# From attention to gating in a four-layer image kernel: `w1` and image 0's first norm moved ahead of a branch, cross terms in one instruction, three more places for image loads

## The chip, the cores and the metric

The kernel runs on one core of one Trainium2 chip. The core has a matrix engine (TensorE, PE in the profile), a vector engine (VectorE, DVE), a scalar engine (ScalarE, ACT), GpSimd (POOL) and a sync engine (SyncE, SP) that issues most of the transfers between device memory (HBM) and the core's own memories: SBUF for operands, and PSUM, into which PE writes its products. Each engine runs its own list of instructions in order, and waits on semaphores for the others. The metric is the device time of one execution in microseconds (us). All tensors are f32.

## The reference, cut to what matters

The input `x` is 8 images of 384 channels of 32x32 points. Four layers follow each other, and each adds its result to its input; a group norm `_gn` (32 groups of 12 channels, per image) stands ahead of each layer.

```python
x = x + _L0(_gn(x))     # attention; ends with a batch norm over all 8 images
x = x + _L1(_gn(x))     # gated layer: 4 experts
x = x + _L2(_gn(x))     # depthwise and pointwise convolution with ternary weights
x = x + _L3(_gn(x))     # deformable attention

# layer 0, the end
out = einsum('bhnm,bhcm->bhcn', attn, v)
out = einsum('oc,bchw->bohw', w_out, out)
return (out - m) * rsqrt(v + EPS) * g + b      # m, v: of each channel, over all images

# layer 1
scores = softmax(x_flat @ gate_w + gate_b, -1)       # 4 experts for every point
top_v, top_i = top_k(scores, 2)
top_w = softmax(top_v, -1)
wmap = top_w.T.reshape(2, b, h, w)
present = (top_i[:, :, None] == arange(4)[None, None, :]).any(0)
coef = einsum('ke,kbhw->ebhw', present, wmap)
hdn = relu(einsum('bchw,edc->ebdhw', x, w1) + b1)
y = einsum('ebdhw,eod->ebohw', hdn, w2) + b2
out = einsum('ebohw,ebhw->bohw', y, coef)
```

Two things follow from this. The batch norm of layer 0 needs the projected output of all eight images, so the group norm of layer 1 can't be had for any image before the last attention product is done. And `present` is taken over all points of all images: the gates of all images must be known before any expert's coefficient is.

## The kernel before

**Tiles.** The 384 channels are 3 chunks of 128 partitions, the 1024 points are a row, taken in two halves of 512 (`HALF`). [...]`x` and the attention's projected output `o` lie in HBM; an image's `x` or `o` in SBUF takes 1.57 MB, and five such places exist (pool `im`, L209).

**The attention stage** (L672 to L951) goes through the images, head pairs and halves. For each image, `out_project` (L746) multiplies by `w_out` (tile `wo0`), copies the product `po` to `ot`, takes its statistics (`bn_stats` into `ost`) and stores it to `o`; it also loads `xh`, the same half chunk of `x`. `cross` (L665) then takes the sum over points of (x - mean of x) times o: a multiply of two tensors on DVE, and a sum over its result (L668); for the second half, `moments` puts the statistics together. From mean and variance of x (`xmv`), of o (`omv`) and the cross term (`xo`), the group statistics of x + batch norm(o) can be worked out without another pass over the data. The last image's second half is projected at the end of the stage (tiles `pos`), its crosses come last (`ends`). During the last image, five image tiles are loaded ahead (`fetch`, L723): x and o of images 0 and 1, and x of image 2.

**The range test** (L942 to L951). `rec` holds the 1024 columns of reciprocals of the softmax sums. One test of all of them against two bounds gives a flag, `bad`; a product with ones (`pok`) adds it up over partitions.

**The norms** (`norms`, L966 to L1002). In order on DVE, with POOL and PE in between: the batch norm's scale and shift (`bn_params`, L159; the reciprocal root is one POOL instruction, `rsqrt`, L98), the channel means summed, a product that spreads them over each group (`gmean`, L976), the channel variances summed, a second such product (`gvar`, L993), POOL's reciprocal root for all eight images, and `rs1`, `sf1`, `sb1`, scale and shift of the norm for each image and channel.

**The branch** (L1007). Every engine loads the flag `bad` and branches: where the range test failed, everything in the If (L1008 to L1140) computes the attention again in an exact manner. With this input the If is skipped. PSUM is handed from the attention's pools to the gated layer's behind it.

**The gated layer's first part.** Behind the branch come `w1` (2.36 MB) and `b1` (L1180, by `load_w`, issued at L1150), the join of image 0 (`join`, `attended`, L1223: x + o times scale, three DVE instructions of 128x1024), and image 0's hidden products. `layer1` (L1417) makes the work for one image as a list of `units`: `enter` (L1431) applies the norm to one half (ScalarE; tile `h1`, shown as `h`), `hidden` (L1495) makes three products `ph` (L1499) for each of 12 k and relu (L1509). The list is interleaved with the loads and joins of the other seven images and with `logits` (L1234), which multiplies each pair of images by the gate (`plog`, L1239). The gate weights themselves, scaled by each image's norm, are built by `gating` (L1203).

**What sets the order.** A scheduler orders each engine's instructions by priorities that follow the order of the program text, unless `issue_after` holds an instruction behind another. SP has one in-order list: a transfer whose place is not free holds up all that are issued behind it. The image loads are issued by `fetch_next` (L1250) from a list, one or two at a time, into whichever of the five places comes free; `w2`, `b2` and the weights of layer 3 (`wq3`, `wk3`, `wv3` and smaller ones) are issued behind the last image load.

**The second part.** With all logits, `route` (L1255) makes the two softmaxes and `present` on DVE, the weights go through HBM (`w0d` out, `w0s` back as a row over all partitions, in `spread`, L1450), `coefficients` and `weight` (L1477) make the coefficient tile `cb` on ScalarE and multiply the hidden tiles by it on DVE (L1485), and `result` (L1514) makes the products `y` (L1520) and adds them to x. Two of the three chunks of the second half's normed input (`h1` in `enter`) lie in the two places of `cb`, so a coefficient tile can only be written when the hidden products no longer read them.

Then the images' layers 1 to 3 follow, in which PE is busy throughout.

Of the kernel before, what the change touches and what calls it, by code (L numbers as in the profile page):

```python
# [13 lines left out]
N = H * W  # L14
# [41 lines left out]
def tile_kernel(ctx: ExitStack, tc: tile.TileContext, i: dict, out: bass.AP):  # L56
# [102 lines left out]
    def bn_params(g, b, tiles):  # L159

        mv, sc, sh = tiles
        n = mv.shape[1]
        nc.vector.tensor_scalar(sh, mv[:, :, 1], 1e-5, None, ALU.add)
        rsqrt(sc, sh, n)
        nc.vector.tensor_tensor(sc, sc, g, ALU.mult)
        nc.vector.tensor_tensor(sh, mv[:, :, 0], sc, ALU.mult)
        nc.vector.tensor_tensor(sh, b, sh, ALU.subtract)
        return sc, sh
# [496 lines left out]
    def cross(b, m, h, xh, ot):  # L665

        nc.vector.scalar_tensor_tensor(xh, xh, xmv[:, b, m, 0:1], ot, ALU.subtract, ALU.mult)
        nc.vector.reduce_sum(xo[:, b, m, h : h + 1], xh, AX.X)  # L668
        if h == 1:
            moments(omv[:, b, m, :], ost[:, m, 2 * b : 2 * b + 2, :])  # L670

    with ExitStack() as pb:  # L672
# [73 lines left out]
        def out_project(b, m, h, po=None):  # L746
            hs = slice(h * HALF, (h + 1) * HALF)
            xh = op.tile([P, HALF], F32, tag="xh", name=f"xh{b}_{m}_{h}")
# [13 lines left out]
            ot = op.tile([P, HALF], F32, tag="ot", name=f"ot{b}_{m}_{h}")  # L762
# [8 lines left out]
            cross(b, m, h, xh, ot)  # L771

        def spare(k, h):


            vf = vts[B % 2].rearrange("p t h d -> p (t h d)")
# [91 lines left out]
        for n, (b, pr, h, kc) in enumerate(steps):  # L868
            if kc == 0:
# [9 lines left out]
                if b + 1 == B and pr == 3 and h == 0:  # L879
                    for k in range(3, 5):  # L880
                        fetch(k)
                if b + 1 == B and pr == 2 and h == 1:
# [42 lines left out]
        for k in range(2):  # L925
            qs = slice(k * HALF // 2, (k + 1) * HALF // 2)
            for m in range(KC):
                for c in range(KC):
# [3 lines left out]
                    )  # L932
        ends = [out_project(B - 1, m, 1, pos[m]) for m in range(KC)]
        for m in range(KC):
            first = bn_moments(ost, m, sc_o)
        ends[0]()

        with tc.issue_after(first.ins):
            for end in ends[1:]:
                end()  # L940

        okt = pp.tile([P, B * NU * 16], F32, tag="p", name="okt")  # L942
        recf = rec.rearrange("p u q -> p (u q)")
        with tc.issue_after(turned.ins):
            nc.vector.tensor_scalar(okt, recf, R_LO, None, ALU.is_ge)
        nc.vector.scalar_tensor_tensor(okt, recf, R_HI, okt, ALU.is_le, ALU.mult)
        okm = np_.tile([P, 1], F32, tag="okm", name="okm", bufs=1)
        nc.vector.tensor_reduce(okm, okt, AX.X, ALU.min)
        pok = bank("pok")
        nc.tensor.matmul(pok[:, 0:1], lhsT=ones, rhs=okm, start=True, stop=True)  # L950
        nc.vector.tensor_scalar(bad, pok[:, 0:1], P - 0.5, None, ALU.is_lt)  # L951
# [3 lines left out]
    w0_ctx.close()  # L955
    _, sco, sho = sc_o
    rs1 = const.tile([P, B], F32, name="rs1")
    sf1 = const.tile([P, B], F32, name="sf1")
    sb1 = const.tile([P, B, KC], F32, name="sb1")
    mean_c = const.tile([P, B, KC], F32, name="mean_c")  # L960
    var_c = const.tile([P, B, KC], F32, name="var_c")
    xs_c = const.tile([P, B, KC], F32, name="xs_c")
    sum_g = const.tile([P, B], F32, name="sum_g")
    mean_g = const.tile([P, B], F32, name="mean_g")

    def norms(moments):  # L966
        for c in range(KC if moments else 0):
            bn_moments(ost, c, sc_o)
        bn_params(gbo[:, 0, :], gbo[:, 1, :], sc_o)
        sc, sh = (t.unsqueeze(1).to_broadcast([P, B, KC]) for t in (sco, sho))  # L970
        nc.vector.tensor_tensor(mean_c, omv[:, :, :, 0], sc, ALU.mult)
        nc.vector.tensor_tensor(mean_c, mean_c, xmv[:, :, :, 0], ALU.add)
        nc.vector.tensor_tensor(mean_c, mean_c, sh, ALU.add)
        nc.vector.reduce_sum(sum_g, mean_c, AX.X)
        pg = bank("gmean")
# [1426 lines left out]
```

## Time and profile before

| | us |
|---|---|
| runs (three) | 3414.34, 3416.99, 3419.63; median 3416.99 |
| profiled execution | 3421.18, its span 3419.1 |
| PE busy | 3321.6 (97%) |
| DVE busy | 1776.3 (52%) |
| ACT busy | 1299.8 (38%) |
| POOL busy | 204.1 (6%) |

HBM is read for 146.33 MB and written for 75.59 MB. The mean granted clock of PE is 0.991 of full speed.

Times below are us from the start of the span. In the list of groups, a row names the line, the engine, the operation, what it writes and reads, the shape, and how many; then the busy time, the mean of one in ns, and, behind the second bar, the idle time of the engine just before these instructions with what ended most of it. In the list of waits, a row says which group of instructions waited for which, and then the sum of the waits in us, their number, and the longest. "SPq" or "DVEq" is the sequencer of an engine, "issue" a time in which an engine waited for nothing that the profile shows. Records of a branch carry the line of the If (L1008).

### The profile page before, as it was taken

To read this page: it belongs to the slowest core of one execution; us is meant where nothing else is said; L and a number is where in the kernel's file an instruction comes from. 1 tells how busy PE (TensorE), PEld (TensorE's weight loads), DVE (VectorE), ACT (ScalarE), POOL (GpSimd) and SP (SyncE) were. 2 spreads that over 40 slices of the span, in tenths; PEclk is the share of its full clock that TensorE was granted. 3 is DMA by queue.
4 is the path that set the end of the run, shared out by engine and by line. 5 is a ranking of instruction groups with operands and counts; after the bars stand their busy time and mean duration, and the time that the engine had idled before them with its cause. 6 is when DMAs were issued, how large, how long until landed. Compare 5 with 4: busy or idle time off the path is not lost.

```text
span 3419.1 us, 44835 instructions
## 1 busy us (share of the span) xinstructions
PE 3321.6 (97%) x18479; PEld 1440.5 (42%) x18479; DVE 1776.3 (52%) x2982; ACT 1299.8 (38%) x1519; POOL 204.1 (6%) x237
## 2 busy tenths in 40 slices
PE   6989999999999999999799999999999999999989
PEld 2433434343434343434344444444444444444444
DVE  8852232323232323234466585565855658658765
ACT  4655444444444444434112332223322232222341
POOL 2110000000000000000000110201102011020121
PEclk9999999999999999999899999999999999999999
DMA  9983121212121111112710010101101011010000
GB/s 355 292 230 81 26 81 26 73 34 66 41 58 49 54 52 50 57 46 74 291 58 22 36 40 27 58 28 36 40 29 57 28 36 40 33 53 27 0 19 38
DMA packets 86979, 234.56 MB, mean 69 GB/s; under 512 B 21880, under 2 KB 22104, under 8 KB 79850
## 3 DMA queue, kind: packets, MB, share of 16 engines
q1 hardware_dynamic: 84602, 223.30, 20.4%
q10 hardware_dynamic: 1248, 4.72, 0.4%
q8 instruction: 149, 2.44, 0.3%
q0 software_dynamic: 912, 3.53, 0.3%
q14 instruction: 68, 0.56, 0.0%
HBM read 146.33 MB, written 75.59 MB: 65 GB/s over the span
## 4 chain that ended last, share of the span: by engine, by line
PE 49%; DVE 2%; ACT 0%; DMA 0%; POOL 0%; issue 0%; DVEq 0%; SPq 0%; POOLq 0%; ACTq 0%
PE y L1520 14%; PE ph L1499 14%; PE pf L2030 4%; PE pq L1682 3%; PE pw L1653 3%; PE pav L1902 3%; PE s L1876 2%; PE pk L1847 1%; DVE off L1778 1%; PE pv L1858 1%; PE xsb L1828 1%; PE pw_last L2091 1%; PE xs L1828 0%; PE px L1742 0%; PE plog L1239 0%; PE pom L1709 0%
## 5 line engine op out<-in xcount | busy, mean ns | idle before, releaser
L827 ACT ACTIVATE p<-s 128x1024 f32<-128x1024 f32 x512 | 496.3, 1021 | 365.7 <-PE s L820 365.5
L1499 PE MATMUL ph<-h,w_sb 128*128 128x512 f32 x1104 | 490.0, 599 | 15.5 <-DMA b_sb<-in_b_dram 14.9
L835 PE MATMUL pav<-p,vt 64*64 64x512 f32 x4096 | 494.9, 588 | 0.0
L1520 PE MATMUL y<-hd,w_sb 128*128 128x512 f32 x1080 | 485.4, 597 | 2.2 <-DVE hd L1485 2.2
L820 PE MATMUL s<-qk,qk 48*64 48x512 f32 x2944 | 355.3, 592 | 0.0
L1499 PEld LDWEIGHTS ph<-h,w_sb 128*128 128x128 f32 x1104 | 208.9, 191 | 273.6 <-issue 270.1
L1520 PEld LDWEIGHTS y<-hd,w_sb 128*128 128x128 f32 x1080 | 199.2, 190 | 233.2 <-issue 221.2
L796 DVE COPY ta<-pav 128x512 f32<-128x512 f32 (+1 forms) x65 | 44.3, 682 | 475.0 <-PE pav L835 475.0
L835 PEld LDWEIGHTS pav<-p,vt 64*64 64x64 f32 x4096 | 168.9, 133 | 272.8 <-issue 272.8
L1509 ACT ACTIVATE hd<-ph,b_sb 128x512 f32<-128x512 f32 x180 | 122.6, 681 | 267.1 <-PE ph L1499 267.1
L574 PE MATMUL pk<-xs,cws_sb 32*32 32x496 f32 (+3 forms) x3840 | 179.6, 604 | 41.0 <-DMA xs<-in_xs_dram 24.7
L1778 DVE SCALAR_TENSOR_TENSOR off<-q,dw_sb,off 128x225 f32<-128x225 f32 (+4 forms) x441 | 215.5, 543 | 2.6
L1641 DVE SCALAR_TENSOR_TENSOR y<-h,tap,y 128x961 f32<-128x961 f32 (+1 forms) x168 | 203.2, 1230 | 0.5
L820 PEld LDWEIGHTS s<-qk,qk 48*64 48x64 f32 x2944 | 109.6, 133 | 210.9 <-issue 190.0
L81 DVE COPY qk<-pq 128x512 f32<-128x512 f32 x46 | 31.8, 692 | 251.9 <-PE pq L258 251.9
L1893 ACT ACTIVATE p<-s 128x1024 f32<-128x1024 f32 x96 | 93.4, 1021 | 161.8 <-PE s L1876 152.6
L1485 DVE TENSOR_TENSOR hd<-hd,cb 128x512 f32<-128x512 f32 x180 | 122.6, 686 | 46.4 <-ACT hd L1509 37.9
L574 PEld LDWEIGHTS pk<-xs,cws_sb 32*32 32x32 f32 (+1 forms) x3840 | 78.4, 111 | 140.6 <-issue 54.6
L1962 POOL TENSOR_TENSOR p<-p,p 128x1024 f32<-128x1024 f32 x48 | 113.7, 2368 | 325.2 <-ACT p L1893 266.8
L2030 PE MATMUL pf<-att,wp_sb 128*128 128x512 f32 x288 | 131.3, 601 | 0.0
L820 PE MATMUL s<-ql,ql 48*64 48x512 f32 x1024 | 128.4, 592 | 0.2 <-ACT p L827 0.2
L711 PE MATMUL pv<-wv_sb,g 128*128 128x384 f32 x384 | 127.1, 489 | 0.0
(369 smaller groups left out, 3744.6 us busy)
## 6 DMA issues: line engine op xcount, KB each, us to landing
rqk<-y SPq DMA_DIRECT2D x96, 256.0 KB
g<-rqk SPq DMA_DIRECT2D x96, 256.0 KB
xs<-in_xs_dram SPq DMA_DIRECT2D x56, 384.0 KB
g<-rv SPq DMA_DIRECT2D x48, 256.0 KB
xh<-in_x_dram SPq DMA_DIRECT2D x48, 256.0 KB
f<-in_x_dram SPq DMA_DIRECT2D x24, 512.0 KB
f<-o SPq DMA_DIRECT2D x24, 512.0 KB
o<-ot SPq DMA_DIRECT2D x42, 256.0 KB
```

The costliest lines, as they stand in the source:

```text
L574: nc.tensor.matmul(banks[r][cols[q]].rearrange("p (h w) -> p h w", w=W)[:, :, c0:c1], lhsT=cws[rs, c, 2 * h + g, x, w], rhs=src[rs, :, c0 ...
L711: nc.tensor.matmul(pv[:, :C], lhsT=acts[b][2][:, c, t * P : (t + 1) * P], rhs=w_in[2][:, c, :], start=(c == 0), stop=(c == KC - 1),)
L820: nc.tensor.matmul(s[64 * k : 64 * k + 64, j * HALF : (j + 1) * HALF], lhsT=kt[r, k0 : k0 + 64], rhs=qt[r, h * HALF : (h + 1) * HALF], sta ...
L827: nc.scalar.activation(p, s, AF.Exp, scale=scale)
L835: nc.tensor.matmul(pav[k][64 * j : 64 * j + 64, :], lhsT=vts[b % 2][r, kc, 2 * hd : 2 * hd + 2, :].rearrange("p a b -> p (a b)"), rhs=p[r, ...
L1485: ahead["hd"] = nc.vector.tensor_tensor(hd, hd, state["cb"], ALU.mult)
L1499: ahead["ph"] = nc.tensor.matmul(ph, lhsT=w1[:, e, c, dc * P : (dc + 1) * P], rhs=state["h1"][c], start=(c == 0), stop=(c == KC - 1),)
L1509: nc.scalar.activation(hd, ph, AF.Relu, bias=b1[:, k : k + 1])
L1520: nc.tensor.matmul(y, lhsT=w2[:, e, dc, m * P : (m + 1) * P], rhs=state[h, k], start=(k == 0), stop=(k == NE * KC - 1),)
L1641: nc.vector.scalar_tensor_tensor(d, f, tap2[:, c, t : t + 1], d, ALU.mult, ALU.add)
L1778: nc.vector.scalar_tensor_tensor(d, f, dw3[:, t : t + 1], d, ALU.mult, ALU.add)
L2030: nc.tensor.matmul(pf, lhsT=wp3[:, pr, m * P : (m + 1) * P], rhs=att[:, pr, hs], start=(pr == 0), stop=(pr == NPAIR3 - 1),)
```

## The change

The edits, in the order of the diff:

- `bn_params` returns its first instruction, so that others can be placed behind it. `cross` becomes one instruction with a second output, the sum over its columns (`accum_out`); `cross_end` adds the `moments`.
- `norms` becomes a generator that stops at points where other work can be placed. It computes all eight images up to the group variance, and then only image 0's `rs1`, `sf1`, `sb1`; `norms_left` does the other seven, behind the branch. The tiles move up to the constants.
- In the last half's projection, the third chunk's `xh` and `ot` lie in memory that is free by then (the attention output of image 6, and a `p` tile). `spare`, another user of free memory, also moves there from a value tile.
- The range test is cut in two: `in_bounds(0)` takes the 896 columns of images 0 to 6, at the second head pair of image 7; `in_bounds(1)` takes the last 128 columns. `pok` adds both.
- The last crosses are placed: cross 0 behind the first instruction of `bn_params`, crosses 1 and 2 behind the sum of means.
- Ahead of the branch: a new pool `h` with `w1` (four transfers), `b1` and the first half's normed image 0 (`h_first`); the first half of image 0's join, one chunk behind each of the variance's sum, the addition of epsilon, and the last instruction of the norm; and the norm itself (`enter_first`). If the If is entered, it does these again. The gated layer's PSUM pools are opened ahead of the branch too, and the If uses them.
- Behind the branch: `join` of image 0 takes the second half only; image loads get named places, the five `im` tiles and three more: `w2`'s memory, the memory of `wq3`, `wk3`, `wv3`, and the three `flat` tiles. Two tables (`NEXT`, `BEHIND`) say which load is issued where. `w2` is loaded behind the last image load as before; `wq3`, `wk3` and `wv3` are loaded behind `w0s`, in the second part.

```diff
@@ bn_params
-        nc.vector.tensor_scalar(sh, mv[:, :, 1], 1e-5, None, ALU.add)
+        begun = nc.vector.tensor_scalar(sh, mv[:, :, 1], 1e-5, None, ALU.add)
...
-        return sc, sh
+        return begun
@@ cross
-        nc.vector.scalar_tensor_tensor(xh, xh, xmv[:, b, m, 0:1], ot, ALU.subtract, ALU.mult)
-        nc.vector.reduce_sum(xo[:, b, m, h : h + 1], xh, AX.X)
+        nc.vector.scalar_tensor_tensor(
+            xh, xh, xmv[:, b, m, 0:1], ot, ALU.subtract, ALU.mult,
+            accum_out=xo[:, b, m, h : h + 1],
+        )
+
+    def cross_end(b, m, h, xh, ot):
+        cross(b, m, h, xh, ot)
         if h == 1:
             moments(omv[:, b, m, :], ost[:, m, 2 * b : 2 * b + 2, :])
+    def norms(bank, moments=False):
...
+        yield bn_params(gbo[:, 0, :], gbo[:, 1, :], sc_o)
...
+        summed = nc.vector.reduce_sum(sum_g, mean_c, AX.X)
+        pg = bank("gmean")
+        nc.tensor.matmul(pg[:, :B], lhsT=g4, rhs=sum_g, start=True, stop=True)
+        yield summed
...
+        summed = nc.vector.reduce_sum(sum_g, var_c, AX.X)
+        pg = bank("gvar")
+        nc.tensor.matmul(pg[:, :B], lhsT=g4, rhs=sum_g, start=True, stop=True)
+        added = nc.vector.tensor_scalar(sum_g, pg[:, :B], 1.0 / KC, 1e-5, ALU.mult, ALU.add)
+        rsqrt(rs1[:, 0:1], sum_g[:, 0:1], 1)
+        nc.vector.scalar_tensor_tensor(
+            sf1[:, 0:1], mean_g[:, 0:1], -1.0, rs1[:, 0:1], ALU.mult, ALU.mult
+        )
+        last = nc.vector.scalar_tensor_tensor(
+            sb1[:, 0, :], sho, rs1[:, 0:1], sf1[:, 0:1].to_broadcast([P, KC]), ALU.mult, ALU.add
+        )
+        yield summed, added, last
+
+    def norms_left():
+        rsqrt(rs1[:, 1:], sum_g[:, 1:], B - 1)
...
@@ out_project
+            third = po is not None and m == 2
+            xh = atts[B - 2][:, 2, :HALF] if third else op.tile(
...
+            ot = pp.tile([P, N], F32, tag="p", name="ot_third")[:, :HALF] if third else op.tile(
...
+        def in_bounds(k):
+            r = slice(k * cut, cut + k * NU * 16)
+            okt = atts[B - 2][:, 2, r]
+            nc.vector.tensor_scalar(okt, recf[:, r], R_LO, None, ALU.is_ge)
+            nc.vector.scalar_tensor_tensor(okt, recf[:, r], R_HI, okt, ALU.is_le, ALU.mult)
+            nc.vector.tensor_reduce(okm[:, k : k + 1], okt, AX.X, ALU.min)
...
                 if b + 1 == B and pr == 3 and h == 0:
                     for k in range(3, 5):
                         fetch(k)
+                    in_bounds(0)
@@ the end of the attention stage
+        with tc.issue_after(turned.ins):
+            in_bounds(1)
         ends = [out_project(B - 1, m, 1, pos[m]) for m in range(KC)]
...
+        with tc.issue_after(next(normed).ins):
+            ends[0]()
+        with tc.issue_after(next(normed).ins):
             for end in ends[1:]:
                 end()
...
+        gvar_at = next(normed)
@@ ahead of the branch
+    hp = ctx.enter_context(tc.tile_pool(name="h", bufs=1, reuse_waits="tile"))
+    w1, b1 = (hp.tile(list(i[nm].shape), F32, name=f"{nm}_sb") for nm in ("w1", "b1"))
+    nc.sync.dma_start(out=b1, in_=i["b1"])
+    for e in range(NE):
+        nc.sync.dma_start(out=w1[:, e], in_=i["w1"][:, e])
+    h_first = hp.tile([P, KC, HALF], F32, tag="h1", name="h1_0_0")
...
+    def enter_first():
         for c in range(KC):
+            nc.scalar.activation(
+                h_first[:, c, :], fetched[0, 0][:, c, :HALF], AF.Identity,
+                bias=sb1[:, 0, c : c + 1], scale=rs1[:, 0:1],
             )
-    norms(False)
+    for c, ins in enumerate(gvar_at):
+        with tc.issue_after(ins.ins):
+            attended(chunks(fetched[0, 0]), chunks(fetched[0, 1]), slice(0, HALF), (c,))
+    enter_first()
+    mm_ctx.close()
+    ps_v = ctx.enter_context(tc.tile_pool(name="ps_v", bufs=1, space=PSUM, reuse_waits="tile"))
+    ps_f = ctx.enter_context(tc.tile_pool(name="ps_f", bufs=3, space=PSUM, reuse_waits="tile"))
@@ behind the branch
-    w1, b1 = load_w("w1"), load_w("b1")
+    norms_left()
...
+    HOMES = {
+        "w2": lambda name: [w2_room[:, c * N : (c + 1) * N] for c in range(KC)],
+        "w3": lambda name: [
+            t.rearrange("p c n -> p (c n)")[:, :N] for t in (wq3, wk3, wv3)
+        ],
+        "flat": lambda name: [pl.flat([P, N], f"{name}_{c}") for c in range(KC)],
+        "im": lambda name: chunks(image(name)),
+    }
...
+            if late and h == 0:
+                state["h1"] = chunks(h_first)
+                return
@@ the main sequence
     units = layer1(pl, 0, True)
+    for at in ((2, 1, "w2"), (3, 0, "w3"), (3, 1, "flat")):
+        fetch_next(*at)
     join(0)
+    fetch_next(4, 0, "im")
     units.pop(0)()
     gating()
-    fetch_next(1)
+    NEXT = {1: (4, 1, "im"), 2: (5, 1, "w2"), 3: (6, 1, "flat"), 4: (7, 1, "im")}
+    BEHIND = {1: ((5, 0, "im"),), 3: ((6, 0, "im"), (7, 0, "w3"))}
     for b in range(1, B):
         join(b)
-        fetch_next(min(1, len(later)))
+        if b in NEXT:
+            fetch_next(*NEXT[b])
...
-            fetch_next(min(1 if b == 1 else 2, len(later)))
+            for at in BEHIND.get(b, ()):
+                fetch_next(*at)
...
+            if k == 2:
+                with tc.issue_after(ahead["spread"].ins):
+                    for n, t in (("wq3", wq3), ("wk3", wk3), ("wv3", wv3)):
+                        load_w(n, t)
```

## The prediction

> **What bounds the kernel now.** I read the page first: TensorE (PE) is busy for 97% of the span, and its large groups wait for nothing, so only a stretch in which PE stands still can pay. One group has such a wait:
>
> ```profile
> L1499 PE MATMUL ph<-h,w_sb 128*128 128x512 f32 x1104 | 490.0, 599 | 15.5 <-DMA b_sb<-in_b_dram 14.9
> ```
>
> 14.9 of its 15.5 us of waiting is one wait for a transfer. The list of who waited for whom, for PE from 1560 to 1790 us, shows what else stands in that stretch:
>
> ```profile
> PE ph L1499 <- DMA b_sb<-in_b_dram: 14.9, 1, 14.9
> PE gmean L976 <- DVE var_c L984: 7.1, 1, 7.1
> PE y L1520 <- DVE hd L1485: 2.2, 1, 2.2
> PE gvar L993 <- DVE sum_g L991: 1.2, 1, 1.2
> ```
>
> The first, second and fourth are one hole, between the last attention product (1621.6) and the first product of the gated layer (1645.93): 24.3 us. The third is 80 us later. The chain that ended last, from 1590 to 1735 us (start, length, what), tells what the end of the hole hangs on:
>
> ```profile
> 1637.05 0.36 SPq L1150
> ...
> 1637.46 8.29 DMA b_sb<-in_b_dram
> 1645.75 0.18 issue
> 1645.93 10.74 PE ph L1499 x18
> 1656.67 2.71 PE plog L1239 x24
> ```
>
> `w1` (2.36 MB), and `b1` behind it, are asked for at 1637.05, after the branch, and take 8.3 us. PE then runs without a hole until 1704.2. Why SyncE (SP) asks so late is in the records of the branch (duration in ns, time of the record):
>
> ```profile
> L1008 ACTq COMPARE_BRANCH  x1: 58/58/58, 1624.1 to 1624.1; - x1
> ...
> L1008 ACTq EVENT_SEMAPHORE  x1: 17/17/17, 1624.6 to 1624.6; - x1
> L1008 PEldq COMPARE_BRANCH  x1: 3571/3571/3571, 1631.1 to 1631.1; - x1
> ...
> L1008 DVEq COMPARE_BRANCH  x1: 72/72/72, 1633.8 to 1633.8; - x1
> ...
> L1008 DVEq EVENT_SEMAPHORE  x1: 21/21/21, 1637.0 to 1637.0; - x1
> ```
>
> VectorE (DVE) reaches the branch at 1633.8, when the norms of all images are done, and is behind it at 1637.0; SP waits 9.0 us for that. So the end of the hole is norms, DVE's 3.2 us over the branch, `w1`.
>
> **The change, step by step.** *`w1` and `b1` ahead of the branch.* They lie where attention's input weights and its first value tile were. SP's order puts `b1` and four transfers of `w1` behind `xh` of the last half's second chunk, whose place is free at 1609.5 (its holder's cross begins at 1608.72 and takes 0.73). In the old load 2.36 MB took 8.3 us; from 1610 they land before 1620. DMA moved 0 to 203 GB/s from 1610 to 1620 and PE reads other memory: 0 us of cost. What sets the hole's end is then the norm of image 0, followed now.
>
> *Statistics.* ScalarE's last copy of the output still ends at 1622.26. Behind it DVE has statistics (0.69), aggregation (0.58) and small operations to L163: 1623.95, before 1626.27. Gain 2.3: three crosses, two sums and 3.1 us of the range test no longer stand ahead. The moved test: 896 of its 1024 columns lie now in the last image's second pair (about 2.7 us, by 1.22 for 1024 twice and 0.65), where DVE has 2.3 us idle and 1.4 us saved from two sums before the next copy that PE needs: covered, 1 us to spare; 128 columns remain.
>
> *To the mean.* GpSimd (POOL) and hand-overs 1.13 (1626.27 to 1627.40, as before), then 1.1 to the sum of means: 1626.2. One cross lies in POOL's gap.
>
> *Crosses in one instruction.* No row of DVE writes a second output. Bounds: the multiply alone, 0.74, or both old ones, 0.74 + 0.69 = 1.43. [...] The two crosses stand ahead of the mean's use: 1628.0; the mean's product (0.75 with hand-overs) lies under them. All other crosses are in the attention stage, where PE waits 0.0: nothing.
>
> *To the variance.* Nine small operations, six in a row at 0.2 (before five took 1.03): 1.35, to 1629.35. Product and hand-overs 0.75, half a chunk of image 0's join (0.65) under it: 1630.1. One addition 0.25, POOL for one value 0.55 (its 128x1 rows; 1.64 for eight before): 1630.9. Two small operations 0.4: 1631.3.
>
> *The first norm.* Three chunks on ScalarE at 0.72 (2.22 for three): 1631.4 to 1633.6. Join chunks two and three (0.65 each) lie beside POOL and the first chunk.
>
> *The branch.* PE's first product now waits for ScalarE behind the branch. PE's own branch begins after the variance's product and is over at 1633.8. ScalarE loads the flag (0.85, begun with the last chunk's dispatch at 1632.9) and needs 0.5 from branch to record: 1634.3; PE at 1634.5. [...]
>
> So the first step: 1645.93 - 1634.5 = 11.4 us. PE is at half clock in its first 5.3 us either way (the granted clock is 0.50 from 1626 on), so that loss stays.
>
> *Image loads and three more places.* Eleven loads of 1.57 MB (17.3 MB) begin when DVE is over the branch: 1635.3 instead of 1641.4. At the 418 GB/s that a full queue moves they take 41 us, to 1677, or 1686 if `w2` and the small weights behind them share. The gates' last product comes 55 us after PE's start, near 1690, its last join 3.8 earlier. Hidden, 0 us. Gate and first joins: DVE is behind the branch at 1635.3, the gate is ready near 1640 and image 1's join at 1643.8; PE wants them at 1645.2. Hidden. The seven other norms (POOL about 1.5, five small DVE operations) lie in there. `wq3`, `wk3`, `wv3` come later by some 20 us; the trace uses the first at 1864.
>
> *The 2.2 us at L1520.* ScalarE's order has the first coefficient ahead of the last hidden chunk. In the trace it began at 1726.17, behind that chunk; the memory it overwrites is read by PE until about 1724.7. Its data come by a transfer issued at 1719.72 behind 0.59 MB; in the new order 0.52 MB stand there. Gain between 0 (data land only at 1726) and 2.1 (nothing but PE holds); 1.4 by the memory's release.
>
> Sum: 11.4 + 1.4 = 12.8 us. Profiled span 3419.1 to 3406.3; with the 2.1 around it 3421.2 to 3408.4. The median of the runs is 4.2 below the profiled execution: 3417.0 - 12.8 = **3404.2**.
>
> **Rivals.** *ScalarE stalls at the branch* as DVE does: PE at 1637.2, 2.7 more, 3406.9. Against: 0.5 in the trace. [...]
>
> *`w1` is still late*, so the move doesn't do what it says: its transfers stand in one queue behind `xh` loads. If they left only after the first late cross (1624.9), they would land at 1633.2, still covered; the start slips at most to 1636, 3405.7. Against: the cross that is waited for ended at 1609.5.
>
> *Logits wait for images.* The old loads took from 1641.4 to 1700.3, 294 GB/s. At that rate the last join ends at 1698 rather than 1677 to 1690, and PE loses 8: 3412. For: loads five and nine onwards still wait in SP's queue for the gate's first and second products. Against: the empty stretches of the old stream were waits for places, and between them it was full:
>
> ```profile
> 1658.00:1660.00 2.00, 2.00 (x18) 0.62 (x11) 1.59 (x2) 0.00 (x0) 0.00 (x0) 1.00 0.00 0
> ...
> 1680.00:1682.00 2.00, 2.00 (x6) 0.87 (x5) 2.00 (x2) 0.69 (x1) 0.00 (x0) 1.00 1.02 418
> ```
>
> (The last three columns of a stretch are PE's clock, DMA's share and GB/s.)
>
> *Slower*: place, the last gating product; price, all that the 17.3 MB need beyond 51 us (1635.3 to the last join at 1686.5). At 271 GB/s the gain is gone, below 245 it is over 0.2% slower; at 230 the loss is 24, 3428. A queue that stops on a place held by a PE product, which itself waits for a load behind it, would do this.
>
> **How the numbers follow.** 0.2% is 6.8 us, about what a measurement here tells from no change. Likeliest case 0.66: 3404.2, own range 3401 to 3407 (L1520 gives 2.1: -0.7; no accumulator read: -0.3; flag load 0.5: -0.35; the cold stretch shifts by up to 1.5 either way; L1520 gives 0: +1.4; crosses at 1.43: +1.4). Stall at the branch 0.14, late `w1` 0.05: with it they make faster 0.85. Logits wait, same within 0.2%: 0.09. Slower 0.06. With all dear ends together (2.7 + 1.4 + 1.4) the branch case ends at 3409.7. Range 3401 to 3410.
>
> **What would show it.** `w1` landed before 1620, no wait of PE for `b_sb`; a hole of 13 us that ends near 1634.5 on ScalarE's `h`; DVE at L163 near 1624; a cross near 0.9 in all; ScalarE's branch to record near 0.5; DMA full from 1637 to 1680 with no waits of `plog`; y starting at most 0.8 us behind the last ph. Wrong if PE starts after 1638, if `plog` waits for joins, or if PE has new holes after 1790, where I expect none, since its order there is the same.

## The result, and the profile after

The changed kernel takes 3406.61 us (median of eight runs, 3403.79 to 3408.20), the kernel before 3416.73 (eight runs, 3414.34 to 3419.63): a ratio of 0.9969, 95% interval 0.9958 to 0.9980. In a second comparison it was 3405.79 against 3418.74, 0.9957 (0.9943 to 0.9970). The forecast was 3404.2, a gain of 12.8 us; the two medians give 10.1 and 12.9. Both lie beyond the 0.2% (6.8 us) that the prediction took for what can be told from no change.

The profiled execution of the changed kernel took 3404.20 us, its span 3402.4. Its page, the two large groups whose waits the prediction started from (columns as on the page of before):

```profile
L1584 PE MATMUL ph<-h,w_sb 128*128 128x512 f32 x1104 | 487.3, 596 | 4.3 <-ACTq L1080 4.1
L1605 PE MATMUL y<-hd,w_sb 128*128 128x512 f32 x1080 | 485.4, 597 | 0.8 <-DVE hd L1570 0.8
```

The first product of the gated layer (`ph`) waited 14.9 us for `b1` before; now it waits 4.1 us, and for the branch. `y` waits 0.8 instead of 2.2. The list of waits of PE, 1560 to 1790 us:

```profile
PE gmean L700 <- DVE sum_g L698: 4.8, 1, 4.8
PE ph L1584 <- ACTq L1080: 4.1, 1, 4.1
PE gvar L718 <- DVE sum_g L716: 2.1, 1, 2.1
...
PE y L1605 <- DVE hd L1570: 0.8, 1, 0.8
```

The first three and the two small products between them (0.57 each) are the whole hole, 12.2 us; no wait for a transfer is left in it. The chain that ended last, from 1590 to 1735 us (start, length, what), has the same pieces as before with the load gone:

```profile
1631.70 9.70 PE ph L1584 x18
1641.40 2.71 PE plog L1312 x24
...
1709.47 0.82 ACT cb L1566
...
1710.31 0.70 DVE hd L1570
...
1711.06 23.44 PE y L1605 x54
```

PE starts at 1631.70, 12.2 us after the last attention product (1619.54); before it was 24.3 us. The records of the branch (duration in ns, then the time of the record) show what that start hangs on:

```profile
L1080 PEldq COMPARE_BRANCH  x1: 3667/3667/3667, 1627.6 to 1627.6; - x1
...
L1080 ACTq COMPARE_BRANCH  x1: 58/58/58, 1630.5 to 1630.5; - x1
L1080 PEldq EVENT_SEMAPHORE  x1: 51/51/51, 1631.3 to 1631.3; - x1
L1080 ACTq EVENT_SEMAPHORE  x1: 17/17/17, 1631.6 to 1631.6; - x1
L1080 DVEq EVENT_SEMAPHORE  x1: 21/21/21, 1632.8 to 1632.8; - x1
```

PE's own skip takes 3.67 us and is over at 1631.3; ScalarE is behind the branch at 1631.6, with the end of its last norm chunk. DVE, for which SP and so everything waited before, comes at 1632.8, and nobody on the path waits for it. SP's list, in which `w1` now leaves at 1608.41, 24.6 us before the first image load (the profile shows `w2`'s memory, into which `o` of an image is loaded there, as `w_sb` too):

```profile
1608.41 2.03 SPq L1046 DMA_DIRECT2D w_sb<-in_w_dram  x4
1632.97 1.57 SPq L1336 DMA_DIRECT2D w_sb<-o  x3
```

Single profiles differ by chance, so both kernels were profiled twice. The table cuts each into pieces, in us:

| piece | before, first | before, second | after, first | after, second |
|---|---|---|---|---|
| start to the end of the last attention product | 1621.62 | 1618.58 | 1619.54 | 1617.65 |
| hole: from there to the first `ph` | 24.31 | 23.62 | 12.16 | 13.37 |
| first `ph` to first `plog` (18 products) | 10.67 | 10.79 | 9.63 | 10.06 |
| first `plog` to the end of the last gating product and hand-over | 48.47 | 48.47 | 48.46 | 48.46 |
| from there to the first `y` | 22.68 | 22.67 | 21.27 | 22.91 |
| first `y` to the end | 1691.35 | 1691.07 | 1691.34 | 1693.05 |

From the last attention product to `y` it is 106.1 and 105.6 before, 91.5 and 94.8 after: 12.7 us less on average. The first row moves by 3.0 us between two profiles of the same kernel. It does hold edits (the 45 other crosses, the moved test), but from the first product of the attention's projections to the last attention product it is 1396.0 and 1395.7 us before, 1396.1 and 1394.4 after: no gain that stands out from the spread. The 1.7 us more in the last row of the second profile after have a cause, told with that profile below.

### The profile page after: what moved, and what is told of

Same layout as the page of the kernel before. It is cut to its first block, busy times and chain, and to the rows that moved or that the text cites. A ratio compares the mean times of both kernels' runs of the same rounds, so it can differ in the third digit from the quotient of the medians.

```text
span 3402.4 us, 44870 instructions
## 1 busy us (share of the span) xinstructions
PE 3323.7 (98%) x18481; PEld 1447.5 (43%) x18481; DVE 1749.1 (51%) x2990; ACT 1300.0 (38%) x1519; POOL 205.1 (6%) x238
## 4 chain that ended last, share of the span: by engine, by line
PE 49%; DVE 2%; ACT 0%; POOL 0%; issue 0%; DMA 0%; DVEq 0%; POOLq 0%; ACTq 0%
PE y L1605 14%; PE ph L1584 14%; PE pf L2115 4%; PE pq L1767 3%; PE pw L1738 3%; PE pav L1987 3%; PE s L1961 2%; PE pk L1932 1%; DVE off L1863 1%; PE pv L1943 1%; PE xsb L1913 1%; PE pw_last L2176 1%; PE xs L1913 0%; PE px L1827 0%; PE plog L1312 0%; PE pom L1794 0%
```

## The experiments

Times of kernels that ran together are compared with the runs of before made beside them. "Hole" and "wait of `y`" are from each kernel's profile.

| kernel | median us | before beside it | ratio (95%) | hole | wait of `y` |
|---|---|---|---|---|---|
| before again | 3417.58 | 3417.88 | 0.9999 (0.9990-1.0008) | 23.6 | 2.2 |
| `w1` alone | 3412.11 | 3417.88 | 0.9981 (0.9972-0.9990) | 18.6 | 2.2 |
| `w1` in its old memory | 3413.79 | 3417.88 | 0.9989 (0.9980-0.9998) | 22.1 | 1.6 |
| first norm behind the branch | 3410.01 | 3417.88 | 0.9972 (0.9961-0.9983) | 14.6 | 3.3 |
| changed kernel again | 3405.79 | 3418.74 | 0.9957 (0.9943-0.9970) | 13.4 | 2.4 |
| five places for images | 3403.28 | 3418.74 | 0.9957 (0.9943-0.9971) | 12.1 | 1.0 |
| only ScalarE's norm behind | 3407.14 | 3418.74 | 0.9965 (0.9951-0.9978) | 14.0 | 2.2 |
| no branch | 3409.92 | 3418.74 | 0.9975 (0.9965-0.9984) | 17.4 | 0.1 |
| crosses in two instructions | 3406.96 | 3417.98 | 0.9966 (0.9952-0.9979) | 13.8 | 2.7 |
| range test in one piece at the end | 3405.61 | 3417.98 | 0.9958 (0.9944-0.9971) | 12.2 | 1.6 |
| no branch, order kept | 3404.96 | 3417.98 | 0.9962 (0.9948-0.9975) | 10.8 | 3.2 |
| `w0s` first in the queue | 3402.89 | 3417.98 | 0.9953 (0.9940-0.9967) | 13.0 | 0.1 |

### Both kernels once more

> The kernel before, unchanged, for a second profile. In the first profiles the stretch from the end of the last attention product (pok) to the first product y took 106.1 us before (1621.6 to 1727.75) and 91.5 us after (1619.5 to 1711.06), 14.6 us less, while the medians of eight runs differ by 10.1 us. Theory A: this stretch is the same in every run, and the rest differs by chance in the first 225 us, where the first profiles already differ by 2.2 us: then it is 106.1 again, within 0.5. Theory B: the first profile of before was long in this very stretch: then it is near 102, and the true gain of the stretch is near 10.

The stretch was 105.6 us: theory A held for the stretch, and the start of it moved from 1621.6 to 1618.6. Of these 3.0 us, 2.7 stand before the first product of the attention's projections (225.6 and 222.9), where no edit is.

> The changed kernel, unchanged, for a second profile. A second profile of the kernel before gave 105.6 us from the last attention product to y (106.1 in the first): so the gain in this stretch is real. Theory A: it repeats, 91.5 within 0.5 us, and the medians come nearer to a difference of 14 than the first 10.1. Theory B: something ahead of the stretch is slower in the changed kernel by some 3 us on average, and eats part of the gain: then the last attention product ends near 1622 in a middling run (1618.6 and 1621.6 in two profiles of before), and the medians stay near 10 apart.

Neither theory was right as written. The stretch was 94.8, not 91.5 within 0.5, and nothing ahead of it was slower (the last attention product ended at 1617.65). The list of waits of this second profile, and PE's records of the branch:

```profile
PE ph L1584 <- PEq L1080: 5.3, 1, 5.3
...
PE y L1605 <- DVE hd L1570: 2.4, 1, 2.4
```

```profile
L1080 PEldq COMPARE_BRANCH  x1: 4816/4816/4816, 1625.9 to 1625.9; - x1
...
L1080 PEldq EVENT_SEMAPHORE  x1: 51/51/51, 1630.8 to 1630.8; - x1
```

The same skip of PE took 4.82 us instead of 3.67 and now ends the hole alone; and `y` waited for its operand even longer than in the kernel before. No edit lies between the two profiles: both are chance, and a median mixes such executions.

The wait of `y` cost more than its length. A stretch of each profile of the changed kernel, the first and then the second, some 2 us behind the first `y` (the busy time of PE, PEld, DVE, ACT and POOL, then PE's granted clock, DMA's share and GB/s):

```profile
1713.00:1715.00 2.00, 2.00 (x6) 0.83 (x5) 2.00 (x4) 0.93 (x2) 0.00 (x0) 1.00 0.17 64
```

```profile
1714.00:1716.00 2.00, 2.00 (x4) 0.81 (x3) 2.00 (x5) 1.01 (x2) 0.00 (x0) 0.50 0.12 47
```

In the second the clock fell to half, and the first 20 products `y` took 10.4 us from start to start instead of 8.7: that is the 1.7 us in the last row of the table. The times of `y` go the same way in all 14 profiles: where `y` waited 2.4 us or more (2.4, 2.7, 3.2 and 3.3 us), its first 54 products took 25.1 us; in the ten in which it waited 2.2 us or less, they took 23.4 us, 1.6 to 1.7 less. The first profile of before, with a wait of 2.2 us, shows the clock at 1.00 in the 9 us behind it.

### `w1` alone, and all but `w1`

```diff
 (kernel before)
+    hp = ctx.enter_context(tc.tile_pool(name="h", bufs=1, reuse_waits="tile"))
+    w1, b1 = (hp.tile(list(i[nm].shape), F32, name=f"{nm}_sb") for nm in ("w1", "b1"))
+    nc.sync.dma_start(out=b1, in_=i["b1"])
+    for e in range(NE):
+        nc.sync.dma_start(out=w1[:, e], in_=i["w1"][:, e])
...
-            vf = vts[B % 2].rearrange("p t h d -> p (t h d)")
+            vf = atts[B - 2].rearrange("p c n -> p (c n)")
...
-    w1, b1 = load_w("w1"), load_w("b1")
```

> The kernel before with one part of the change alone: w1 and b1 in memory of their own, asked for ahead of the branch (and spare's memory moved as in the change, to free theirs). My theory: w1 is only the last of several things in the hole; with it gone the hole ends when DVE is behind the branch (1637.0), the first join chunk (1.25) and ScalarE's first norm chunk (0.8) are done: PE starts at 1640.0 of that profile, 18.4 us after the last attention product instead of 24.3, 5.9 us gained, time near 3411. Rival: the load is the hole, and this part alone brings what the whole change brought (hole near 12, 10 us or more gained).

Hole 18.56, against 18.4 expected; the median is 5.8 us below that of before, against 5.9. The rival falls. The list of waits of this kernel's PE:

```profile
PE ph L1503 <- ACT h L1449: 9.0, 1, 9.0
PE gmean L981 <- DVE sum_g L979: 6.9, 1, 6.9
PE y L1524 <- DVE hd L1489: 2.2, 1, 2.2
```

With the transfer gone, PE waits 9.0 us in one piece for ScalarE's `h`, which waits for the join on DVE behind the branch.

```diff
 (changed kernel)
-    w1, b1 = (hp.tile(list(i[nm].shape), F32, name=f"{nm}_sb") for nm in ("w1", "b1"))
-    nc.sync.dma_start(out=b1, in_=i["b1"])
-    for e in range(NE):
-        nc.sync.dma_start(out=w1[:, e], in_=i["w1"][:, e])
...
     pl = Pools(pd, "d")
+    w1, b1 = load_w("w1"), load_w("b1")
     norms_left()
```

> The changed kernel with w1 and b1 back in their old memory behind the branch; all else stays. My theory: SP then waits again for DVE to be over the branch (1632.8 in the profile after), w1 takes its 8.3 us, PE starts near 1641.4 instead of 1631.7: hole 21.9 instead of 12.2, 9.7 us lost, and the image loads stand behind w1 and begin 5 us later, which costs nothing more. Rival: the other edits alone shorten the hole, and w1's load overlaps the norm that is now ahead of the branch: under 5 us lost.

Hole 22.07, against 21.9 expected. The chain of this kernel:

```profile
1631.11 8.04 DMA b_sb<-in_b_dram
1639.15 0.15 issue
1639.30 2.90 PE ph L1581 x3
```

All the faster norms are in this kernel, and PE still stands for 22 us: everything in the hole is one chain (norms, DVE over the branch, `w1`), and an edit pays only as far as the next link. From 24.0 us (mean of two profiles of before), `w1` alone takes 5.4 away, all the rest alone 1.9, both together 11.2 (to the mean of 12.2 and 13.4).

### The first norm behind the branch

```diff
 (changed kernel)
-    for c, ins in enumerate(gvar_at):
-        with tc.issue_after(ins.ins):
-            attended(chunks(fetched[0, 0]), chunks(fetched[0, 1]), slice(0, HALF), (c,))
-    enter_first()
...
     pl = Pools(pd, "d")
+    attended(chunks(fetched[0, 0]), chunks(fetched[0, 1]), slice(0, HALF))
+    enter_first()
     norms_left()
```

> The changed kernel with image 0's first half joined and normed behind the branch again; w1 stays ahead. My theory: DVE is over the branch at 1632.8, one join chunk of 128x512 (0.75) and one norm chunk on ScalarE (0.72) follow: PE starts near 1634.6 instead of 1631.7, 2.9 us lost. ScalarE's list has the first coefficient tiles behind the last hidden chunk here, as in the kernel before: if that order is what took the wait of y from 2.2 to 0.8 us, 1.4 more are lost, 4.3 in all. Rival: DVE's way over the branch gets shorter without the join ahead of it, and nothing is lost in the hole.

Hole 14.60: 2.4 us lost against the first profile of the changed kernel, 2.9 expected. DVE's row shows where it stands until it may join:

```profile
1632.79 2.08 DVE L1052 SCALAR_TENSOR_TENSOR f<-f,bnsc_out,f 128x512 f32<-128x512 f32 x3 [3.59 <-DVEq L1076]
```

This kernel's wait of `y` was 3.3 us; its `w0s` stood behind 1.05 MB of x in SP's queue instead of 0.52. It also gave, unasked, a price for something else. POOL's reciprocal root for one value, here with no join beside it on DVE:

```profile
1628.19 0.55 POOL L98 TENSOR_TENSOR rs<-sum_g,mhalf 128x1 f32<-128x1 f32 x1 [4.80 <-DVE sum_g L719]
```

0.55 us, the estimate of the prediction. In the changed kernel the same instruction took 0.99 with a 128x512 join on DVE beside it, as the rows of POOL and then of DVE in the profile after show:

```profile
1621.76 1.28 POOL L98 TENSOR_TENSOR bnsc_out<-bnsh_out,mhalf 128x3 f32<-128x3 f32 x1 [1380.77 <-DVE bnsh_out L163]
1627.85 0.99 POOL L98 TENSOR_TENSOR rs<-sum_g,mhalf 128x1 f32<-128x1 f32 x1 [4.81 <-DVE sum_g L719]
```

```profile
1621.51 0.17 DVE L163 TENSOR_SCALAR bnsh_out<-bnmv_out 128x3 f32<-128x3 f32 x1
1621.59 0.74 DVE L667 SCALAR_TENSOR_TENSOR xh<-xh,xmv,ot 128x512 f32<-128x512 f32 x1
1622.26 0.08 DVE L667 DVE_READ_ACCUMULATOR xh<-xh,xmv,ot 128x1 f32 x1
...
1627.69 0.74 DVE L1052 SCALAR_TENSOR_TENSOR f<-f,bnsc_out,f 128x512 f32<-128x512 f32 x1
1628.88 0.16 DVE L721 SCALAR_TENSOR_TENSOR sf<-mean_g,rs 128x1 f32<-128x1 f32 x1 [0.44 <-POOL rs L98]
```

The three-column root is longer too: 1.28 us with a cross of two inputs beside it (1621.59 above; 1.28 again with crosses in two instructions and with no branch and the order kept, where the rows show the same cross), 0.85 in the first profile of the kernel before, where a one-input sum runs beside it (L668, 0.69 us from 1626.39; the root starts at 1626.52). The differences are 0.44 us for one column and 0.43 for three; these rows show their size and not their cause.

```diff
 (changed kernel: the three activations of enter_first alone)
-    enter_first()
...
     pl = Pools(pd, "d")
+    enter_first()
     norms_left()
```

> The changed kernel with ScalarE's three norm chunks behind the branch, DVE's join of the first half still ahead. In the profile after, ScalarE's first record behind the branch falls together with the end of its last chunk (1631.6), PE's own at 1631.3. Theory A: ScalarE's branch only waits for its own last chunk; put ahead of them it is over long before, and PE starts when its own branch is done, 0.3 us earlier (hole near 11.9). Theory B: ScalarE stalls over the branch as DVE does, some 3 us, hidden behind nothing here: it is over by 1625 all the same, so the hole is equal too, but the gap between its branch and its next record shows 3 instead of 0.5. ScalarE's and SP's orders at the first y are as in the run with the whole norm behind, so y waits near 3.2 instead of 0.8: 2.1 us lost in all.

Both theories fell on the hole, and `y` waited 2.2 us, not 3.2. ScalarE was over the branch at 1620.3, 0.5 us after its branch record, and still did not start:

```profile
1631.44 2.22 ACT L1062 ACTIVATE h<-f,sb,rs 128x512 f32<-128x512 f32 x3 [12.61 <-DVEq L1079]
```

In brackets stand the idle time ahead of it and what ended it: DVE's sequencer at the branch. The first activation behind the branch reads what DVE has written, and here it waited until DVE was behind the branch too, at 1631.3, though the data were there at 1628.1. It was not a wait for all engines: in the first profile of the changed kernel PE starts at 1631.70, 1.1 us before DVE is over the branch. Hole 13.98 instead of 12.16. Here the place ahead of the branch counted for the consumer (1.8 us of the hole) as well as for the producer.

### Crosses and range test

```diff
-        nc.vector.scalar_tensor_tensor(
-            xh, xh, xmv[:, b, m, 0:1], ot, ALU.subtract, ALU.mult,
-            accum_out=xo[:, b, m, h : h + 1],
-        )
+        nc.vector.scalar_tensor_tensor(xh, xh, xmv[:, b, m, 0:1], ot, ALU.subtract, ALU.mult)
+        nc.vector.reduce_sum(xo[:, b, m, h : h + 1], xh, AX.X)
```

> The changed kernel with each cross as two DVE instructions again. The accumulator read took 0.08 us in the profile after, a cross 0.67 from start to start. Theory A: crosses 1 and 2 stand ahead of the mean's use and cost 0.6 us more each: from the last attention product to the first product of the gated layer 1.2 us more (13.4 where PE's branch takes 3.7, 14.5 where it takes 4.8); the 45 other crosses cost nothing. Theory B: they lie beside POOL's and PE's hand-overs, and nothing is lost.

Hole 13.78 with a skip of 3.5 us on PE: 1.6 more than 12.16, against 1.2 expected. Theory A holds, with 0.4 us on top. DVE's rows of crosses 1 and 2:

```profile
1624.39 0.74 DVE L667 SCALAR_TENSOR_TENSOR xh<-xh,xmv,ot 128x512 f32<-128x512 f32 x1
1625.05 0.74 DVE L667 SCALAR_TENSOR_TENSOR att<-att,xmv,ot_third 128x512 f32<-128x512 f32 x1
1625.71 0.68 DVE L668 TENSOR_REDUCE xo<-xh 128x1 f32<-128x512 f32 x1
1626.31 0.67 DVE L668 TENSOR_REDUCE xo<-att 128x1 f32<-128x512 f32 x1
```

Four instructions stand ahead of the mean's use, from 1624.39 to 1626.90, 2.51 us; in the profile after two stood there, from 1624.14 to 1625.47, 1.33. That is 1.2; the other 0.4 is the sum of cross 0 (0.68), which slips in front of the channel means: their sum ends 0.5 us later behind the last attention product. The one-instruction form took 0.67 from start to start, and the multiply alone 0.66 (1624.39 to 1625.05): the record of the accumulator's read (0.08 us, in the fence of DVE above) added 0.01 us at most.

```diff
@@ last image, head pair 3
                     for k in range(3, 5):
                         fetch(k)
-                    in_bounds(0)
@@ end of the attention stage
         with tc.issue_after(turned.ins):
+            in_bounds(0)
             in_bounds(1)
@@ in_bounds
-            okt = atts[B - 2][:, 2, r]
+            okt = pp.tile([P, N], F32, tag="p", name=f"okt{k}")[:, r]
```

> The changed kernel with all 1024 columns of the range test behind the last transposes again. The 896 columns moved back take 2.7 us of DVE (0.57 + 1.07 + 1.07, by length from 0.65, 1.22 and 1.22 for 1024). Theory A: in the profile after DVE then stands idle for 2.5 us, until ScalarE has copied the first of the last products; the test fills that gap: 0.2 us lost at most. Theory B, as my prediction counted it: the test stands ahead of the statistics and 2 us or more are lost.

Hole 12.16, to the hundredth the one with the test cut in two: theory A. DVE's rows:

```profile
1614.41 0.72 DVE L855 TENSOR_SCALAR okt<-rec 128x896 f32<-128x896 f32 x2
1615.05 1.28 DVE L856 SCALAR_TENSOR_TENSOR okt<-rec,okt 128x896 f32<-128x896 f32 x2
1616.25 1.27 DVE L857 TENSOR_REDUCE okm<-okt 128x1 f32<-128x896 f32 x2
1617.73 0.70 DVE L841 BATCH_NORM_STATS2 ost<-po 128x6 f32<-128x512 f32 x1 [0.21 <-ACT ot L840]
```

The whole test (1614.41 to 1617.52) ends 0.21 us before the statistics may begin, which wait for ScalarE's copy. Moving it gained nothing in the hole.

### Five places for images

```diff
-    for at in ((2, 1, "w2"), (3, 0, "w3"), (3, 1, "flat")):
-        fetch_next(*at)
     join(0)
-    fetch_next(4, 0, "im")
     units.pop(0)()
     gating()
+    fetch_some(1)
...
-        if b in NEXT:
-            fetch_next(*NEXT[b])
+        fetch_some(min(1, len(later)))
...
-            for at in BEHIND.get(b, ()):
-                fetch_next(*at)
+            fetch_some(min(1 if b == 1 else 2, len(later)))
```

`fetch_some` takes the next loads of a list, all of them into the pool `im`.

> The changed kernel without the three more places: image loads in the five old places, one or two at a time as in the kernel before. Theory A (as I put it: hidden): the first load starts when the second half of image 0 is joined (1637), each later one when a join or a gating product frees a place; at 3.8 us for 1.57 MB the last lands near 1681, its join ends near 1685, PE wants it at 1686.1: nothing lost in the gating, at most 2 us. Theory B: the loads keep the 59 us that they took before (1641.4 to 1700.3): last join near 1697, PE waits some 9 us for logits, 9 us lost.

Theory A: from the first gating product to the hand-over behind the last it is 48.49 us, against 48.46 with eight places. DVE's rows, the last join and the copy of the logits:

```profile
1684.20 3.68 DVE L1052 SCALAR_TENSOR_TENSOR f<-f,bnsc_out,f 128x1024 f32<-128x1024 f32 x3 [5.00 <-DMA f<-o]
1690.23 0.69 DVE L1342 COPY ls<-plog 128x512 f32<-128x512 f32 x1 [2.35 <-PE plog L1312]
```

The last join ends at 1687.88, 0.5 us after the last gating products have begun (1687.35, with its first chunk): there is no slack left. With eight places the last join ends at 1680.3 and PE wants it at 1686.1. The three places bought 5.8 us of slack and no time.

### No branch

```diff
-    redo = nc.values_load(bad[0:1, 0:1], min_val=0, max_val=1)
-    with tc.If(redo > 0):
-        with ExitStack() as pb:
...
```

> The changed kernel without the branch and without what it guards: the exact recomputation for inputs outside the range test is left out. Theory A: PE's first gated product then waits for the first norm chunk alone (its end 1630.1), 1.5 us earlier: hole near 10.7; DVE's 3.5 us at the branch fall away and are hidden anyway: 1.5 us gained. Theory B: the branch's 4 us on PE and 3 us on DVE are on the path: 4 us gained.

Slower, by 4 us against the changed kernel beside it (3409.92 and 3405.79), with a hole of 17.4. DVE's rows name the reason:

```profile
1628.45 1.28 DVE L1052 SCALAR_TENSOR_TENSOR f<-f,bnsc_out,f 128x1024 f32<-128x1024 f32 x1
...
1629.84 1.27 DVE L1052 SCALAR_TENSOR_TENSOR f<-f,bnsc_out,f 128x1024 f32<-128x1024 f32 x1
...
1631.13 1.27 DVE L1052 SCALAR_TENSOR_TENSOR f<-f,bnsc_out,f 128x1024 f32<-128x1024 f32 x1
```

Three joins of image 1 (1.3 us each) stand between the instructions of image 0's variance. Three joins of image 0's second half (0.75 us each, from 1624.53 on) slipped in ahead of them, and later an instruction that waits 1.3 us for the root of the seven other images. The branch had kept them all behind; without it the scheduler fills DVE's list with work that is ready, in front of work that PE waits for.

```diff
+    normed_at = gvar_at[2].ins
...
+    with tc.issue_after(normed_at):
+        norms_left()
```

The last instruction of image 0's norm holds back the joins, `gating` and the clearing of the gate in the same way.

> The changed kernel without the branch and the exact recomputation behind it, now with the joins, the gates and the other images' norms held behind image 0's norm, as the branch held them (without that they slipped in between on DVE and cost 5 us). Theory A: PE's first gated product waits for the first norm chunk alone: hole near 10.7 us; against 12.2 and 13.4 in the two profiles of the changed kernel that makes the branch's price 1.5 to 2.7. Theory B: it is PE's branch record, 3.4 to 4.8 us, in full: hole near 9.

Hole 10.78, against 10.7 expected. PE's list of waits:

```profile
PE y L1469 <- DVE hd L1434: 3.2, 1, 3.2
PE ph L1448 <- ACT h L1062: 2.7, 1, 2.7
```

PE waits for ScalarE's first chunk alone (2.7). So the branch costs 1.4 to 2.6 us of the hole, not the 3.4 to 4.8 that PE's skip takes: the rest lies beside the norm. Its `y` waited 3.2 us for its operand, and the median shows no gain.

### `w0s` first in the queue

```diff
-            load_image(xt, x_img[b])
+            with tc.issue_after(ahead["spread"].ins) if b == 1 else nullcontext():
+                load_image(xt, x_img[b])
```

> The changed kernel with the loads of x of image 1 held behind the transfer of w0s. In the two profiles of the changed kernel y waited 0.8 and 2.4 us: in the second ScalarE waited 2.6 us for w0s, issued behind 0.52 MB of x. Theory A: with nothing ahead in the queue w0s lands before the memory of the coefficient tile is free, and y waits 0.8 each time: up to 1.6 us gained. Theory B: it is the transfer's own length, 512 KB written over all partitions, and y waits between 0.8 and 2.4 as before.

`y` hardly waited (0.06 us), less than theory A's 0.8. ScalarE's row of the first coefficient tile:

```profile
1710.49 1.59 ACT L1567 ACTIVATE cb<-w0s,prs,dp 128x512 f32<-128x512 f32 x2 [0.26 <-DMA w0s<-w0d]
```

It begins 4.35 us after `w0s` is issued (1706.14); in the two profiles of the changed kernel it was 5.1 and 6.7 us. Here it begins 1.5 us before PE's last hidden product ends, in the first profile of the changed kernel 0.8 us before: the memory of the tile is free earlier than it was used there. So in the first profile too it was the transfer that held `y`, although the profile puts ScalarE's wait down to PE. The piece from the gating to the first `y` was 20.5 us, against 21.3 and 22.9. By the medians (0.9953 against 0.9957 and 0.9969) it can't be told from the changed kernel.

## Why the prediction was right

**The chain through the norms held, link by link.** In us from the end of the last attention product, forecast and first profile after: L163 2.3 and 2.0; sum of means 4.6 and 4.7; crosses done 6.4 and 6.0; sum of variances 7.7 and 7.3; variance read back 8.5 and 8.1; root done 9.3 and 9.3; first norm begins 9.8 and 9.8, ends 12.0 and 12.1; PE starts 12.9 and 12.2. `w1` left at 1608.4 and had landed by 1617 (DMA moved 401 GB/s from 1614 to 1616, 46 from 1616 to 1618), so it was 0 us of cost, as said.

**Sizes that cancelled.** A cross is 0.67, not 0.90 (0.5 us in all). No run shows the 0.90 that the forecast counts for each cross; the first profile after has a multiply of 0.74, a read of the accumulator of 0.08, and 0.67 from start to start. The one-value root is 0.99, not 0.55, with the join that I laid beside it; the three-column one 1.28 instead of 0.85. The prediction treated "beside POOL" as free; the longer roots cost 0.9 us and took back what the crosses (0.5) and the earlier statistics (0.4 at L163) gave. That the root was done at 9.3 us as forecast is luck.

**Range test: wrong.** "3.1 us of the range test no longer stand ahead" is not so: they stood in a gap of DVE. The gain to L163 (2.7 us) comes from the crosses and sums that no longer stand ahead: with the whole test back at the end, L163 comes 2.0 us behind the last attention product as well.

**The branch: the right place, half the right reason.** I had PE wait for ScalarE's flag load and branch behind its last chunk, 0.9 us. ScalarE loads the flag while its chunks run (at 1630.0; the chunks from 1629.4 to 1631.6), and its first record behind the branch falls on the end of the last one: 0.1. What I had listed as over in time, PE's own skip, ends within 0.3 us of that in the first profile and decides alone in the second. The rival of a stall of ScalarE (0.14) did not come: with its chunks behind the branch, ScalarE was over it in 0.5 us. PE's own skip, 3.57 us in the profile of before, took 3.67 and 4.82, and the prediction gave that term no range.

**The cold stretch** was put at no change; the first 18 products took 9.6 and 10.1 us instead of 10.7 and 10.8. PE had its full clock earlier after its start: the granted clock is 0.50 to 1634, 0.71 from 1634 to 1636 and 1.00 from there, so some 3.5 us behind 1631.7; before it was 0.62 from 1650 to 1652, some 5.6 us behind 1645.9. That is 0.9 us on average, inside the 1.5 that the range allowed, and in the main luck: in the runs with five places and with the test at the end, holes of 12.1 and 12.2 us, the same products took 10.7 and 10.8; the spread over all profiles is 9.4 to 11.0. In the first traces' record of the clock this stretch at half clock lasts 13.65 us after and 27.31 us before, four and eight times the 3.41 us of the shortest such stretch in the trace of before.

**L1520:** 1.4 us were taken "by the memory's release". The first profile shows 1.4, the second none and 1.7 us lost behind it by the clock, and the run with `w0s` first shows that it is the transfer. The lower end, 0 where data land late, was the one with the reason in it; a loss below 0 was not thought of. The sign named for it, `y` at most 0.8 us behind the last `ph`, came in the first profile alone.

**Image loads** were hidden, as forecast, with DMA at 413 to 434 GB/s from 1640 to 1680; the rival of late logits and the slower case fell. That five places hide them too was not forecast: the experiment alone showed it.

On average over two profiles each: hole -11.2 (forecast -11.4), cold stretch -0.9 (0), `y` -0.6 (-1.4), in sum -12.7 (-12.8). That it comes so near is luck in part: 0.9 us of the cold stretch that were not forecast stand in for the 0.8 missing at `y`, and the 1.7 us lost behind the late `y` are in no term. The intervals of both comparisons, 10.1 and 12.9 us by the medians, hold the forecast.

## What to carry to other kernels

Follow a hole as one chain and ask of each edit what the next link is: here the load alone gave 5.4 us, the rest alone 1.9, both 11.2. The branch was a fence here for an engine that reads what another wrote (ScalarE behind DVE, 12.6 us idle in the run with only its norm behind; SP behind DVE, 9.0 us in the kernel before), so work moved ahead of it needs its producers, its memory and its consumers ahead too; and the same fence kept ready work from slipping in front of urgent work. Before counting an instruction's removal as a gain, look whether its engine stood idle right behind it (2.5 us behind the range test here), and before laying it beside POOL, whether it has two inputs (0.4 us a root here). And look at the clock behind a wait of PE: with 2.4 us instead of 2.2 at `y`, 1.7 more were lost here.

## What the runs showed of the hardware

- PE's skip over the branch varied from 3.33 to 4.82 us in twelve profiles (eight of them within 3.33 to 3.67), and was 3.67 and 4.82 in two profiles of the same program; DVE's, from its branch to its next record, from 2.8 to 3.2; ScalarE's took 0.4 to 0.5 in the five in which it had nothing to finish.
- GpSimd's small reciprocal roots took 0.43 to 0.44 us more in the rows with a two-input VectorE instruction beside them: one column 0.55 without (the first norm behind the branch) and 0.99 with it (the changed kernel), three columns 0.85 beside a one-input sum (the kernel before) and 1.28 (the changed kernel).
- PE's granted clock was 1.00 behind waits of `y` of 0.8 us (first profile after) and 2.2 us (first profile of before), and 0.50 from 1714 to 1716 behind a wait of 2.4 us (second profile after). The first 54 products took 23.4 us behind waits of up to 2.2 us (ten profiles) and 25.1 behind waits of 2.4 to 3.3 us (four profiles).
- The sum as a second output of a VectorE multiply (128x512) added a record of 0.08 us; from one instruction to the next it was 0.67 us with it and 0.66 without.
- The transfer of `w0s`, a row of 4 KB to all partitions, took between 4.4 and 7.0 us from its issue to the first use: 4.4 with no image load right ahead of it in the queue, 5.1 to 6.7 with 0.52 MB of x ahead (three profiles), 6.5 and 7.0 with 1.05 MB (two).
